# A node score repeated over the partitions: by TensorE transposes or by two transfers through DRAM

## The chip, the cores and the metric

The kernel runs on one core of a Trainium2 chip. The core has five engines that follow their own instruction streams in order: TensorE (PE; its weight loads are shown apart as PEld), VectorE (DVE), ScalarE (ACT), GpSimd (POOL) and SyncE (SP). SP computes nothing: it issues the transfers (DMAs) between DRAM and the on-chip memory SBUF. TensorE writes its products into PSUM[...]. The metric is the time of one execution in microseconds (us); less is better. The kernel before takes 1116.52 us, the median of three runs (1116.37 to 1117.14).

## The reference

The reference is a stack of four graph layers over 32 graphs of 512 nodes with 128 features, all with one 512 x 512 adjacency matrix `adj`. Each layer normalises its input, applies a relu, runs a graph layer and adds the result to `x`:

```python
h = jnp.maximum(_layernorm(x, axis=-1), 0.0)
x = x + _L0_gnn_ref(h, adj, ...)     # then L1, L2, L3 in the same way
```

Layers 1 and 2 are attention layers. Each node gets two scores, and the score of an edge is the sum of one score of each end. Layer 2, with layer 1 alike up to a weighting by `adj` and an MLP after it:

```python
Wh = jnp.einsum('bnf,fo->bno', h, W)
f1 = Wh @ a1
f2 = Wh @ a2
e = jax.nn.leaky_relu(f1[:, :, None] + f2[:, None, :], negative_slope=ALPHA)
e = jnp.where(adj[None, :, :] > 0, e, NEG_INF)
attention = jax.nn.softmax(e, axis=2)
```

Here `f2[:, None, :]` is the point of this study: one number per node, needed as a row beside every other node. Layer 0 has scores `u1`, `u2` and an index rule that pairs neighbouring nodes:

```python
e = u1[:, idx1] + u2[:, idx2]
e = jnp.where(e >= 0, e, ALPHA * e)
att = jax.nn.softmax(jnp.where(adj > 0, e, NEG_BIG), axis=1)
out = jnp.einsum('bik,bkl->bil', att, h) + x @ self_weight
```

Layer 3 has no scores that depend on the nodes: its attention is computed once from `adj`, and only two products per graph are left.

## The kernel before, in words

All of `x` stays in SBUF for the whole run, as `xs` with 128 partitions, 32 graphs, 4 chunks of 128 nodes and 128 features. Node n of a graph lies on partition n mod 128 of chunk n // 128. The masks made from `adj` (`bias`, `adjT`, `biasT`, `mask2T`, `adjTe`) and the weights stay in SBUF too. The work is one function per layer and graph: `layer0(b)` for all 32 graphs, then `layer1(b)` for all, then `layer2(b)` mixed with `layer3(b - 4)`.

Every layer begins with `preln(b)`: statistics on VectorE (L475, L477), the normalisation on GpSimd (L489, L510), four transposes on TensorE (L386) and a relu copy on ScalarE (L519), which gives `hT`. In layers 0 to 2, `project_scored` (L543) multiplies `hT` by a weight matrix with two more columns, so that `h` (copied by ScalarE at L377) holds 128 features and, in columns 128 and 129, the two scores of each node. A score is then a number on each of 128 partitions, for four chunks.

VectorE needs one of them as a row of 512 values, the same on every partition. `repeated` (L569) makes it with four TensorE transposes of a column that is read 128 times over; the result `prow` is a PSUM bank. In `attend` (layers 1 and 2) the four instructions at L587 add `prow` to the mask `bias`, write `y[0]` to `y[3]` and take the maximum of each row. ScalarE then adds the other score and applies the leaky relu (L612) and the exponential (L620). TensorE transposes the result, VectorE multiplies or copies it into `pT` (L629, L379), and TensorE forms the output `po` (L640). In `layer0` the row is made of `ls`, the leaky relu of the sum of both scores (`sc` and `ls`, L673 and L677, on VectorE). Two times two instructions at L692 add its even or odd nodes to `biasT`. Four transfers from SBUF to SBUF (L664) bring the other pairing of scores, `u`, into place; L702 is its first reader. ScalarE's exponentials are at L742, the scaled features `hs` and `hs2` at L770 and L771, the products at L776 and L784, and the sum into `xs` at L790.

The order of the instructions is found by `Plan` when the kernel is built. Each step is an `op` with an engine, an assumed length, what it reads and writes, and for a transfer its number of DMAs and an assumed load. `Plan.run` repeatedly takes the step that can begin first by these assumptions. Among steps of one engine that could begin within 0.05 us of each other it takes the one with the smaller `turn`, which is its graph's starting time plus four times the assumed length of the way to the step within the graph. After a step's end, 0.22 us (TensorE, ScalarE), 0.15 (VectorE), 0.13 (GpSimd) or 2.2 (SP) pass in the plan before its result can be read. At most seven graph layers are open at a time. Buffers are given out by the plan from pools: eight PSUM banks, five `scored` (for `h`), eight `scores` (for `y`), six `by_act` and others. Eight transfers can be on their way at once. The plan's order is fixed in the program: on each engine the instructions run in that order, so a waiting instruction holds up all that follow it on its engine. This includes SP, where a transfer that waits for its source holds up the transfers behind it.

`load_x(b + 6)` brings in the input of a later graph in layer 0 (L370), and `layer3` sends out the result (L909).

Of the kernel before, what the change touches and what calls it, by code (L numbers as in the profile page):

```python
# [33 lines left out]
P = 128  # L34
# [195 lines left out]
def kernel(  # L230
# [65 lines left out]
    scores = room("scores", 8, (P, C, P))  # L296
    turned = room("turned", 4, (P, C, P))
    spare = room("spare", 9, (P, C, P))

    plan = Plan(tc)  # L300
    op = plan.op
# [264 lines left out]
            )  # L566
        return h

    def repeated(col, reads):  # L569

        prow = value(banks, "prow")
        turn_op(lambda k: prow.t[:, k, :], lambda k: col(k).to_broadcast([P, P]), reads, [prow])
        return prow

    def attend(h, weights, v_weights):


        prow = repeated(lambda k: h[0].t[:, k, P + 1 : P2], h)
        y = [value(scores, "y") for _ in range(C)]
        rmax = Value()  # L580
        top = [Value() for _ in range(C)]
        for ib in range(C):

            def emit(ib=ib):
                if ib == 0:
                    rmax.own = small("rmax")
                nc.vector.tensor_tensor_reduce(  # L587
                    wide(y[ib].t), wide(prow.t), bias[:, ib, :], 1.0, LOWEST, ALU.add, ALU.max,
                    rmax.own[:, ib : ib + 1],
                )  # L590

            op(DVE, 0.61, emit, [prow, v_bias], [y[ib], top[ib]])
        ntop, nmax = Value(), Value()

        def emit_top():
# [56 lines left out]
    def layer0(b):  # L652
# [25 lines left out]

        dve(0.08, emit_sc, h, [sc])
        dve(0.08, emit_ls, [sc], [ls])  # L680
        prow = repeated(lambda k: ls.own[:, k : k + 1], [ls])
        y = [value(scores, "y") for _ in range(H)]
        rmax, top = Value(), [Value() for _ in range(H)]
        for hf in range(H):

            def emit_max(hf=hf):
                if hf == 0:
                    rmax.own = small("rmax")
                node = wide(prow.t).rearrange("p (i q) -> p q i", q=2)
                for k in range(2):  # L690
                    jb = 2 * hf + k
                    nc.vector.tensor_tensor_reduce(  # L692
                        wide(y[hf].t)[:, k * N2 : k * N2 + N2], node[:, hf, :], biasT[:, jb, :], 1.0, LOWEST,
                        ALU.add, ALU.max, rmax.own[:, jb : jb + 1],
                    )

            op(DVE, 0.7, emit_max, [prow, v_biasT], [y[hf], top[hf]])
        lt1, lt, nltm, nmax, ltn = (Value() for _ in range(5))

        def emit_lt1():  # L700
# [548 lines left out]
```

## Time and profile before

| | value |
|---|---|
| median of three runs | 1116.52 us |
| the profiled execution | 1114.53 us |
| its span, first to last instruction | 1112.8 us |
| TensorE, VectorE, ScalarE, GpSimd busy | 98%, 83%, 60%, 60% |
| `prow` on TensorE | 384 transposes, 273 ns each as recorded |
| first and last `prow` of layer 0 | 15.8 and 206.3 us |
| first and last `prow` of layers 1 and 2 | 212.0 and 1068.5 us |
| score instruction of layers 1 and 2 (L587) | 256 of 683 ns |
| score instruction of layer 0 (L692) | 128 of 415 ns |
| traffic of the transfers over the span | 20.50 MB in 56911 packets |

The profile is one execution recorded by the hardware. A group of instructions is written as line, engine, operation and output<-input; "x" is a count. Where instructions of TensorE overlap, the busy time of a group is less than the count times the mean. "SPq" is the issuing of a transfer by SP, and the time to landing of a transfer runs from its issue to the moment its data has arrived. A stage of the run is read from a view that gives every engine's busy time in a stretch of the span.

### The profile page before, as it was taken

How to read it: one execution, taken by the hardware profiler on the slowest of the kernel's cores; microseconds unless marked ns; L12 is line 12 of the kernel's file. 1: busy time of each engine (PE TensorE's matmuls, PEld its weight loads, DVE VectorE, ACT ScalarE, POOL GpSimd, SP SyncE). 2: the span in 40 equal slices, each digit the busy share in tenths (PEclk: the TensorE clock that was granted, in tenths of full speed). 3: DMA queues.
4: the chain of work that ended last, by engine and by line, in shares of the span. 5: the costliest groups of instructions: out<-in, count | busy, mean ns of one | idle time of the engine just before them, and what ended most of it. 6: DMA issues, size and time to landing. Idle time of an engine off the chain costs nothing.

```text
span 1112.8 us, 25144 instructions
## 1 busy us (share of the span) xinstructions
PE 1085.5 (98%) x8680; PEld 989.0 (89%) x8683; DVE 922.5 (83%) x3822; ACT 672.1 (60%) x1588; POOL 673.2 (60%) x1040
## 2 busy tenths in 40 slices
PE   5999999999999999999999999899999999999998
PEld 4899999998787877887788887899999999999997
DVE  8989899978889898998989897977777777777772
ACT  3456455567365565574656765866667766766661
POOL 8355454554546555646456555687776777777773
PEclk8899999999999999999999999999999999999999
DMA  7202210000000000000000000000100000000001
GB/s 189 58 11 50 43 36 2 2 2 2 1 1 1 1 1 1 1 1 1 1 1 2 1 1 1 1 20 20 30 21 20 21 20 20 20 21 29 21 21 39
DMA packets 56911, 20.50 MB, mean 18 GB/s; under 512 B 21584, under 2 KB 56272, under 8 KB 56784
## 3 DMA queue, kind: packets, MB, share of 16 engines
q1 hardware_dynamic: 56784, 18.90, 6.9%
q8 instruction: 69, 1.13, 0.4%
q14 instruction: 58, 0.48, 0.1%
HBM read 10.43 MB, written 8.39 MB: 17 GB/s over the span
## 4 chain that ended last, share of the span: by engine, by line
PE 75%; DVE 16%; ACT 3%; POOL 2%; issue 1%; SPq 1%; DMA 1%; POOLq 0%; ACTq 0%; DVEq 0%
PE po L640 16%; PE pt L386 13%; PE po L784 10%; PE po L901 10%; PE proj L557 6%; PE pg L834 5%; DVE y L587 4%; PE prow L386 3%; PE po L776 2%; ACT y L620 2%; DVE st L475 2%; PE po L897 2%; PE p L535 2%; DVE pT L629 2%; PE pz L535 1%
## 5 line engine op out<-in xcount | busy, mean ns | idle before, releaser
L640 PE MATMUL po<-h,pT 128*128 128x128 f32 x2048 | 244.2, 275 | 1.7 <-DVE pT L379 1.0
L510 POOL TENSOR_SCALAR xn<-xs,nmean,rstd 128x128 f32<-128x128 f32 x512 | 232.0, 469 | 19.7 <-DVE st L475 9.6
L640 PEld LDWEIGHTS po<-h,pT 128*128 128x128 f32 x2048 | 236.3, 192 | 5.8 <-issue 1.9
L620 ACT ACTIVATE y<-y,nmax 128x512 f32<-128x512 f32 x256 | 181.7, 712 | 41.1 <-DVE nmean L501 20.1
L612 ACT ACTIVATE y<-y,h 128x512 f32<-128x512 f32 x256 | 165.4, 712 | 37.4 <-DVE rmax L587 37.1
L489 POOL TENSOR_TENSOR rstd<-ve,mhalf 128x4 f32<-128x4 f32 x160 | 163.9, 1024 | 13.4
L587 DVE CUSTOM_DVE_ANT_0 y<-prow,bias 128x512 f32<-128x512 f32 x256 | 161.9, 683 | 9.5 <-PE prow L386 9.0
L519 ACT ACTIVATE hT<-pt 128x512 f32<-128x512 f32 x128 | 75.5, 591 | 125.0 <-PE pt L386 123.2
L386 PE MATMUL pt<-ident,y 128*128 128x128 f32 x1024 | 135.1, 274 | 2.5 <-ACT y L620 1.8
L901 PE MATMUL po<-h,offT 128*128 128x128 f32 x1024 | 135.4, 275 | 0.5 <-ACT h L377 0.5
L487 POOL TENSOR_SCALAR ve<-mv 128x4 f32<-128x4 f32 x160 | 36.7, 229 | 160.9 <-DVE rsum L756 57.7
L386 PEld LDWEIGHTS pt<-ident,y 128*128 128x128 f32 x1024 | 115.7, 141 | 20.0 <-ACT y L620 11.4
L834 PE MATMUL pg<-adjTe,hg 128*128 128x512 f32 x256 | 128.2, 593 | 0.0
L901 PEld LDWEIGHTS po<-h,offT 128*128 128x128 f32 x1024 | 124.6, 192 | 0.6 <-ACT h L377 0.6
L475 DVE BATCH_NORM_STATS2 st<-xs 128x6 f32<-128x128 f32 x512 | 109.9, 276 | 1.5 <-POOL xs L879 1.4
L557 PE MATMUL proj<-w_ext,hT 128*128 128x130 f32 x768 | 107.8, 279 | 2.3 <-ACT hT L519 2.3
L557 PEld LDWEIGHTS proj<-w_ext,hT 128*128 128x128 f32 x768 | 97.7, 194 | 6.7 <-ACT hT L519 2.9
L377 ACT COPY h<-proj 128x260 f32<-128x260 f32 x192 | 67.6, 371 | 46.3 <-PE proj L557 40.5
L879 POOL TENSOR_TENSOR xs<-xs,em 128x512 f32<-128x512 f32 x32 | 40.9, 1278 | 81.2 <-DVE em L878 81.2
L386 PE MATMUL pt<-ident,xn 128*128 128x128 f32 x512 | 85.2, 279 | 2.7 <-POOL xn L510 1.9
L629 DVE TENSOR_TENSOR pT<-pt,adjT 128x512 f32<-128x512 f32 x128 | 82.1, 680 | 3.4 <-PE pt L386 3.2
L742 ACT ACTIVATE y<-y,nmax 128x256 f32<-128x256 f32 x128 | 63.8, 501 | 31.1 <-DVE rs L760 14.0
(189 smaller groups left out, 2101.2 us busy)
## 6 DMA issues: line engine op xcount, KB each, us to landing
xs<-in_x_dram SPq DMA_DIRECT2D x32, 256.0 KB, 3.6
out_dram<-yo SPq DMA_DIRECT2D x32, 256.0 KB, 2.2
u<-h SPq DMA_DIRECT2D x128, 0.5 KB, 1.8
bias<-in_adj_dram SPq DMA_DIRECT2D x4, 256.0 KB, 3.3
wts<-in_L_gnn_W_dram SPq DMA_DIRECT2D x3, 64.0 KB, 3.8
rows<-in_L_gnn_bias_dram SPq DMA_DIRECT2D x2, 64.0 KB, 3.3
wt_o<-L_gnn_others_weight_dram SPq DMA_DIRECT2D x1, 64.0 KB, 2.3
wts<-n_L_gnn_self_weight_dram SPq DMA_DIRECT2D x1, 64.0 KB, 3.8
```

The lines of the kernel that those rows point to most:

```text
L386: nc.tensor.transpose(dst(k), src(k), ident)
L475: nc.vector.bn_stats(st[:, c, :], src(c))
L489: nc.gpsimd.tensor_tensor(rstd.own, ve, mhalf, ALU.pow)
L510: nc.gpsimd.tensor_scalar(xn.t[:, c, :], src[:, c, :], nmean.own[:, c : c + 1], rstd.own[:, c : c + 1], ALU.add, ALU.mult,)
L557: nc.tensor.matmul(p[:, c, :], lhsT=column(hT, 2 * k + c), rhs=w_ext, start=(b3 is None), stop=(b3 is None or c == 1),)
L587: nc.vector.tensor_tensor_reduce(wide(y[ib].t), wide(prow.t), bias[:, ib, :], 1.0, LOWEST, ALU.add, ALU.max, rmax.own[:, ib : ib + 1],)
L612: nc.scalar.activation(yw, yw, AF.Prelu, alpha=0.2, bias=h[0].t[:, ib, P : P + 1])
L620: nc.scalar.activation(yw, yw, AF.Exp, bias=nmax.own[:, ib : ib + 1], accum_out=ssum[0].own[:, ib : ib + 1])
L640: nc.tensor.matmul(po[ib].t[:, ib, :], lhsT=pT.t[:, jb, :], rhs=h[0].t[:, jb, 0:P], start=(jb == 0), stop=(jb == C - 1),)
L784: nc.tensor.matmul(po[ib].t[:, ib, :], lhsT=w, rhs=(hs if ib < H else hs2).t[:, jb, :], start=False, stop=(jb == C - 1),)
L834: nc.tensor.matmul(wide(pg.t), lhsT=hg.t[:, nb, :], rhs=adjTe[:, nb, :], start=(nb == 0), stop=(nb == C - 1))
L901: nc.tensor.matmul(po[ib].t[:, ib, :], lhsT=offT[:, jb, blk(ib)], rhs=h1.t[:, jb, :], start=False, stop=(jb == C - 1),)
```

## The change

`repeated` goes, and `repeat` comes in its place. It writes the score of the 512 nodes as one line of 2 KB into DRAM with SP, and reads that line back with a second transfer which repeats it over the 128 partitions. The destination is the last of the layer's `y` buffers, not a PSUM bank. The last score instruction then reads and writes the same buffer. For layer 0 the line is written with the even nodes first and the odd ones after (`step` is 2), by two transfers, so that the score instructions read contiguous halves. The DRAM lines come from a pool of eight.

```diff
+    dram = ctx.enter_context(tc.tile_pool(name="dram", bufs=8, space=bass.MemoryType.DRAM))
+    outside = Room(8, lambda n: dram.tile([1, N], F32, name=n, tag="row"))
...
-    def repeated(col, reads):
-
-        prow = value(banks, "prow")
-        turn_op(lambda k: prow.t[:, k, :], lambda k: col(k).to_broadcast([P, P]), reads, [prow])
-        return prow
+    def repeat(col, reads, v_row, step=1):
+
+        line = value(outside, "line")
+
+        def emit():
+            to = line.t.rearrange("o (q c p) -> q p (o c)", q=step, p=P // step)
+            for q in range(step):
+                nc.sync.dma_start(to[q], col()[q:P:step, :])
+
+        op(SP, 0.45 * step, emit, reads, [line], transfers=step)
+        op(SP, 0.45, lambda: nc.sync.dma_start(wide(v_row.t), line.t.to_broadcast([P, N])), [line], [v_row],
+           load=1.0, transfers=1)
...
-        prow = repeated(lambda k: h[0].t[:, k, P + 1 : P2], h)
         y = [value(scores, "y") for _ in range(C)]
+
+        repeat(lambda: h[0].t[:, :, P + 1], h, y[-1])
...
-                    wide(y[ib].t), wide(prow.t), bias[:, ib, :], 1.0, LOWEST, ALU.add, ALU.max,
+                    wide(y[ib].t), wide(y[-1].t), bias[:, ib, :], 1.0, LOWEST, ALU.add, ALU.max,
...
-            op(DVE, 0.61, emit, [prow, v_bias], [y[ib], top[ib]])
+            op(DVE, 0.61, emit, [y[-1], v_bias], [y[ib], top[ib]])
...
-        prow = repeated(lambda k: ls.own[:, k : k + 1], [ls])
         y = [value(scores, "y") for _ in range(H)]
+        repeat(lambda: ls.own, [ls], y[-1], 2)
...
-                node = wide(prow.t).rearrange("p (i q) -> p q i", q=2)
...
-                        wide(y[hf].t)[:, k * N2 : k * N2 + N2], node[:, hf, :], biasT[:, jb, :], 1.0, LOWEST,
+                        wide(y[hf].t)[:, k * N2 : k * N2 + N2], wide(y[-1].t)[:, hf * N2 : hf * N2 + N2], biasT[:, jb, :],
+                        1.0, LOWEST,
...
-            op(DVE, 0.7, emit_max, [prow, v_biasT], [y[hf], top[hf]])
+            op(DVE, 0.7, emit_max, [y[-1], v_biasT], [y[hf], top[hf]])
```

## The prediction

> **What bounds the kernel now.** I read the page's header first, then busy time by stage. I cut the stages where the node row `prow` changes form: `prow<-ident,ls` (layer 0) is last issued at 206.3 us, `prow<-ident,h` (layers 1 and 2) runs from 212.0 to 1068.5. Columns of the stage view: stretch, its length, busy us and instructions of PE, PEld, DVE, ACT, POOL, granted clock, DMA share, GB/s.
>
> ```profile
> PE 1085.5 (98%) x8680; PEld 989.0 (89%) x8683; DVE 922.5 (83%) x3822; ACT 672.1 (60%) x1588; POOL 673.2 (60%) x1040
> ...
> 60.00:211.00 151.00, 151.00 (x1358) 150.79 (x1357) 138.38 (x771) 84.50 (x307) 75.71 (x148) 1.00 0.15 26
> 211.00:672.00 461.00, 456.51 (x3246) 377.68 (x3247) 407.97 (x1599) 279.72 (x608) 249.90 (x345) 1.00 0.00 1
> 724.00:1112.80 388.80, 383.34 (x3394) 376.50 (x3392) 278.72 (x997) 247.97 (x524) 280.01 (x431) 1.00 0.08 23
> ```
>
> TensorE has no free time in any stage. VectorE is second: 92% in layer 0, 88% in layer 1, 72% in layers 2/3. The chain of waits, limited to layer 0, is TensorE alone, the row's transposes among it:
>
> ```profile
> by line: PE po L784 57.2%; PE proj L557 14.4%; PE po L776 14.3%; PE prow L386 7.0%; PE pt L386 6.9%; PE proj L552 0.2%
> ```
>
> In layers 2/3 TensorE's timeline repeats every 13.10 us (prow at 780.24 and 793.34), and the next work starts 0.43 us after a row does:
>
> ```profile
> 793.34 0.60 PE L386 MATMUL prow<-ident,h 128*128 128x128 f32 x4
> 793.77 1.06 PE L535 MATMUL p<-wts,hT 128*128 128x128 f32 x8
> ```
>
> So a row costs TensorE about 0.435 us of its order, not the 4 x 273 ns that the records show, which overlap. Layer 0 repeats every 6.24 us (`h` copied at 115.37, 121.60, 127.84). Last, SP's timeline, since the change puts its work there:
>
> ```profile
> 116.02 2.86 SPq L664 DMA_DIRECT2D u<-h  x4
> 118.93 0.59 SPq L370 DMA_DIRECT2D xs<-in_x_dram  x1
> 122.26 2.55 SPq L664 DMA_DIRECT2D u<-h  x4
> ...
> xs<-in_x_dram SPq DMA_DIRECT2D x32, 256.0 KB, 3.6
> out_dram<-yo SPq DMA_DIRECT2D x32, 256.0 KB, 2.2
> u<-h SPq DMA_DIRECT2D x128, 0.5 KB, 1.8
> ```
>
> The reader should see that one DMA issue holds SP for about 0.635 us (2.55/4), so layer 0 already uses 2.55+0.6 = 3.15 of each 6.24 us of SP.
>
> **What the Trainium skill says.** "DMA: Bandwidth & Descriptors", section on the anatomy of one DMA: a transfer has a fixed cost of about 2 us, most of it the receipt from the memory written, heaviest for HBM. The trace agrees: 1.8 us for 0.5 KB SBUF to SBUF, 2.2 for 256 KB into DRAM. Same page, rules for kernel authors: a DMA that reads what another wrote must wait for its semaphore, and a strided last dimension becomes one descriptor per element. The line is therefore 512 elements of 4 bytes and the second transfer cannot start before the first has landed. Same page, specifications: below 512 B the engine does a read-modify-write. No run of before writes small elements into DRAM. Same page, queues and rings: each engine consumes a ring in order, so a small write queued behind an x load waits for it; u's landing, 1.8 median but 3.7 at most, would fit.
>
> **The change part by part.**
>
> *Removed from TensorE.* 96 rows (32 in each of three layers) x 0.435 = 41.8 us, 13.9 a layer. Every stage is TensorE's, so this is the largest possible gain, if nothing else takes its place. A PSUM bank per row comes free too; I price that at 0, as TensorE does not wait for banks in the steady stages.
>
> *VectorE.* The same 256 + 128 score instructions read SBUF instead of PSUM. Rows with both operands in SBUF: 686 ns (em, L878) to 718 (xs<-res, L855), against 683 now; so 0 to +35 ns, at most 9 us on L587 and some 4 on L692. I take 0; the 8% to 28% of VectorE that is idle hides it, and uncovered it would cost those 13 us. Using the last `y` in place orders the last score instruction behind the others; they run in that order already.
>
> *Added to SP and DRAM.* Layers 1 and 2: one write (0.635 of SP), a wait for landing, one broadcast (0.635). Layer 0: two writes of 256 elements, one broadcast, 3 x 0.635 = 1.9. Landing L of the line: 1.8 (u) to 3.7 (u's worst); I take 2.1, near out's 2.2. Landing of the broadcast, 256 KB into SBUF: 2.2 (out) to 3.6 (x load); I take 2.8. From `h` to the row in place: 2.1 + 2.8 = 4.9 us with no queueing, and 7.3 at the upper ends.
>
> *Who waits.* On VectorE the score instruction waits for the broadcast, and behind it stand the pT products and copies of other layers that TensorE needs. Layers 2/3: `h` is complete at 787.05 (786.23 + 0.82) and its scores start at 795.10: 8.05 us are there already. Layer 1: `h` complete at 524.10 or before, scores at 525.74, but the first half of `h` is copied at 520.04; the order must move by some 3 us, for which five `scored` and eight `scores` buffers leave room at 13.6 us a layer. The plan charges 0.45+2.2+0.45+2.2+1.0 = 6.3 us for the path, so it orders VectorE's work for a later row than my 4.9. In layers 2/3 SP's only other transfer is `out`, whose source is ready at 791.83; the write (787.1) and broadcast (near 789.8) go ahead of it.
>
> *Layer 0 on SP.* The broadcast waits on SP, and behind it are the next layer's four u transfers (for L702) and x load. SP's cycle: four u 2.54, first write 0.635, L from the second write's issue to its landing, broadcast 0.635: 3.81 + L = 5.9 with L = 2.1, if the x load is issued in that wait; 6.55 if it lies elsewhere in the order (only until x's last load at 156 us). TensorE would want 6.24 - 0.435 = 5.8, VectorE 6.24 x 0.92 = 5.7. So SP takes the bound over; at 5.9 for some layers and 6.55 for others, layer 0 gains -0.34 x 16 = -5 and loses 0.3 x 16 = +5. The crowded SP start (35 to 50 us, u transfers back to back) is inside that. I take 0 for layer 0.
>
> *Sum.* Layers 2/3: -13.9, less the ends where TensorE is not full (383.34 of 388.80, and the handover from layer 1): -12.5. Layer 1: VectorE would go from 88.5% to 91%, and its chain passes often between engines; I take two thirds, -9. Layer 0: 0. Total -21.5. The profiled execution ran 1114.53 with a span of 1112.8; this gives a span of 1091.3 and a run near 1093. Its 1.7 us outside the span stay. The median, 1116.52, lies 2.0 above the profiled run, so 1095.
>
> **Rivals.**
> *A. SP becomes the bound of layer 0 and takes more than the rest gives (slower).* If the 4-byte writes into DRAM land in L = 3.6 (as slow as an x load), the cycle is 7.4 with the x load inside, 8.05 outside: +1.2 to +1.8 over 6.24, x 32 = +38 to +58, less 21.5: 1133 to 1153. It decides from 3.81 + L = 6.24 + 21.5/32 = 6.9, that is L = 3.1 (2.5 with the x load outside). For it: SP already spends half of layer 0, and small DRAM writes are unpriced. Against it: the two small landings seen are 1.8 and 2.2.
> *B. VectorE bounds layers 0 and 1 (little gained).* Layer 0 has 0.5 us of VectorE slack in 6.24, layer 1 1.6 in 14.4; a row late by a microsecond eats it. Then only layers 2/3 give: 1116.5 - 12.5 = 1104, and with the 13 us of slower score reads, 1117. For it: VectorE's 92%. Against it: in layers 2/3 it cannot happen at 72%.
> *C. The order changes for the worse.* Longer planned paths defer everything behind the row, by 4 x 4.64 us of planned turn in layers 1 and 2 (0.45+2.2+0.45+2.2 for 0.44+0.22, times the planner's 4), so more layers are open at once and buffers run out; a stall of 0.5 us in each of 96 layers would cost 48 us against the 41.8 saved, about 1122. Nothing in the trace shows buffers short, so little weight.
>
> **How the numbers follow.** Forecast 0.50 (1080 to 1104); A 0.29, slower; B 0.14, 0.10 of it faster and 0.04 within no change; C 0.07, 0.03 unchanged and 0.04 slower. That is faster 0.60, same 0.07, slower 0.33, where 0.2% (2.2 us) is about what a measurement of this kernel can tell. Forecast's own range 1080 to 1104. Up to 1135 takes in B, C and A's lower end; below 1080 (nearly the whole 41.8) I leave 0.06, above 1135 0.13.
>
> **What would show it.** The 13.10 us period of layers 2/3 becomes about 12.67; if it does not, C or a late row holds. The line's landing is near 2.1 us and the broadcast's near 2.8; the 6.24 us of layer 0 becomes 5.9 to 6.5. Line landings above 3 us, SP without pause in layer 0 and TensorE idle before `po` there show A. VectorE above 97% in layer 0 shows B. If scores wait for the broadcast in layers 1 and 2 by more than a microsecond each, my landing prices were wrong and so is the forecast.

## The result and the profile after

The changed kernel takes 1698.76 us, the median of four runs (1695.66 to 1701.41), against 1116.44 us for the kernel before on the same chip. The ratio is 1.521 (95% interval 1.519 to 1.524), so the change costs 582 us where a gain of 21.5 was forecast. The profiled execution took 1699.38 us with a span of 1697.7.

The header of the page of the changed kernel, busy time by engine:

```profile
PE 1235.4 (73%) x8299; PEld 1103.1 (65%) x8299; DVE 935.6 (55%) x3822; ACT 680.1 (40%) x1588; POOL 696.3 (41%) x1040
```

No engine is full any more. TensorE was 98% busy before. It executes 8299 matmuls instead of 8680, and its busy time is nevertheless longer, 1235.4 us for 1085.5. The next view shows the reason. These are stages of the changed kernel, with the columns of the stage view in the prediction: layer 0, then layer 1 with the first graphs of layer 2, then the rest of layers 2/3 from 1300 us on.

```profile
60.00:365.00 305.00, 216.19 (x1431) 199.79 (x1430) 162.62 (x873) 93.79 (x333) 95.78 (x158) 0.81 0.33 42
365.00:1060.00 695.00, 524.73 (x3253) 427.63 (x3254) 435.09 (x1693) 306.57 (x658) 280.57 (x379) 0.86 0.11 15
1300.00:1697.00 397.00, 286.09 (x2137) 278.16 (x2134) 181.63 (x635) 156.69 (x330) 177.29 (x271) 0.85 0.13 27
```

The granted clock (the third number from the end) is 0.81 to 0.86, where it was 1.00 in the stages shown before, and a matmul that is left takes longer: those of `po` from `pT` (L650) take 295 ns, for 275 before. In the profiled runs of this case the mean clock goes with TensorE's busy share: 0.994 at 98% before, 0.931 at 87% and 0.875 at 78% in two kernels of the experiments (`unread`, `l0_turn`), 0.841 at 73% here. That the idle time comes first is seen in experiment 6: with the same instructions in the same order, another shape of the line's write takes the share from 75% to 94% and the clock from 0.861 to 0.985. The second to last number is the share of time that the DMA engines are busy: 11% in layer 1. Little is being moved there while TensorE, VectorE and ScalarE wait.

The last row of layer 0 was begun at 206.3 us before (its transposes) and at 363.8 now (its write), which is 157.5 us later. From there to the end of the span it takes 1333.9 us instead of 906.5, which is 427 more. So about a quarter of the loss is in layer 0 and three quarters come after it. The chain of work that ended last, by line:

```profile
DMA line<-h 20%; DMA y<-line 18%; DMA line<-ls 9%; PE po L650 6%; PE pt L388 5%; PE po L911 4%; DVE y L597 4%; PE proj L559 3%; PE p L537 2%; PE pg L844 2%; DMA u<-h 2%; DVE st L477 1%; POOL xn L512 1%; ACT y L622 1%; ACT h L379 1%
```

Before, layer 0's chain was TensorE alone. Now the three kinds of transfer that the change adds carry 47% of the chain of the whole run, and the write (`line`) weighs more than the broadcast. Who waits for them is in the view of waits. First VectorE's waits (in total us, times, longest):

```profile
DVE y L597 <- DMA y<-line: 388.3, 58, 15.3
DVE y L701 <- DMA y<-line: 95.6, 26, 10.3
DVE lt L712 <- DMA u<-h: 68.5, 16, 8.0
```

Then SP's own waits:

```profile
SPq L581 <- DMA line<-h: 576.4, 64, 12.6
SPq L581 <- DMA line<-ls: 144.1, 27, 8.8
```

In layers 1 and 2, 58 of 64 graphs find VectorE waiting for the row, 6.7 us each. On SP the broadcast (L581) waits for the line, 9.0 us each time in layers 1 and 2. In layer 0 what is queued behind it on SP, the next layer's `u` transfers, comes late as well: that is the 68.5 us of L712.

One graph of layers 2/3 shows the length of the path. SP's timeline (start, duration):

```profile
1228.78 0.36 SPq L578 DMA_DIRECT2D line<-h  x1
1237.38 0.33 SPq L581 DMA_DIRECT2D y<-line  x1
```

and VectorE's timeline at the end of the same path, with the idle time before it in brackets:

```profile
1242.26 0.69 DVE L597 CUSTOM_DVE_ANT_0 y<-y,bias 128x512 f32<-128x512 f32 x1 [6.26 <-DMA y<-line]
```

The line took 8.6 us from its issue until SP could issue the broadcast, and the broadcast another 4.9 us until the row could be used. That is 13.5 us from `h` to the row, against 4.9 forecast, 6.3 assumed by the plan and 7.3 for the two upper ends of my bounds. Behind L597 on VectorE stand the copies and products that TensorE needs; TensorE's next work after this wait was a matmul at 1244.86, after 6.51 us without any: it waited for `hT` from ScalarE, which waited for a VectorE product (`own`) that stands behind L597.

Layer 0 shows the same write on SP's timeline:

```profile
212.42 0.33 SPq L581 DMA_DIRECT2D y<-line  x1
212.84 2.56 SPq L674 DMA_DIRECT2D u<-h  x4
215.50 1.26 SPq L578 DMA_DIRECT2D line<-ls  x2
216.80 0.60 SPq L372 DMA_DIRECT2D xs<-in_x_dram  x1
225.00 0.33 SPq L581 DMA_DIRECT2D y<-line  x1
```

From broadcast to broadcast it takes 12.58 us. SP issues for 4.8 of these and then stands until the line has landed, with nothing of the later layers going past.

### The profile page after: what moved, and what is told of

It reads as the page before. It is cut to its first block, busy times and chain, and to the rows that moved or that the text cites. A ratio compares the mean times of both kernels' runs of the same rounds, so it can differ in the third digit from the quotient of the medians.

```text
span 1697.7 us, 24773 instructions
## 1 busy us (share of the span) xinstructions
PE 1235.4 (73%) x8299; PEld 1103.1 (65%) x8299; DVE 935.6 (55%) x3822; ACT 680.1 (40%) x1588; POOL 696.3 (41%) x1040
## 4 chain that ended last, share of the span: by engine, by line
DMA 50%; PE 27%; DVE 11%; ACT 4%; issue 3%; POOL 3%; SPq 2%; ACTq 0%; DVEq 0%; POOLq 0%
DMA line<-h 20%; DMA y<-line 18%; DMA line<-ls 9%; PE po L650 6%; PE pt L388 5%; PE po L911 4%; DVE y L597 4%; PE proj L559 3%; PE p L537 2%; PE pg L844 2%; DMA u<-h 2%; DVE st L477 1%; POOL xn L512 1%; ACT y L622 1%; ACT h L379 1%
## 5 line engine op out<-in xcount | busy, mean ns | idle before, releaser
L597 DVE CUSTOM_DVE_ANT_0 y<-y,bias 128x512 f32<-128x512 f32 x256 | 174.1, 708 | 389.8 <-DMA y<-line 388.3
L650 PE MATMUL po<-h,pT 128*128 128x128 f32 x2048 | 281.6, 295 | 59.4 <-DVE pT L639 44.0
L650 PEld LDWEIGHTS po<-h,pT 128*128 128x128 f32 x2048 | 270.3, 212 | 67.7 <-DVE pT L639 38.2
L512 POOL TENSOR_SCALAR xn<-xs,nmean,rstd 128x128 f32<-128x128 f32 x512 | 250.6, 503 | 97.2 <-DVE nmean L503 28.9
L559 PE MATMUL proj<-w_ext,hT 128*128 128x130 f32 x768 | 136.3, 328 | 46.7 <-ACT hT L521 46.0
L491 POOL TENSOR_TENSOR rstd<-ve,mhalf 128x4 f32<-128x4 f32 x160 | 164.1, 1026 | 13.3
L388 PE MATMUL pt<-ident,xn 128*128 128x128 f32 x512 | 109.3, 319 | 76.5 <-POOL xn L512 67.5
L559 PEld LDWEIGHTS proj<-w_ext,hT 128*128 128x128 f32 x768 | 124.7, 240 | 56.0 <-ACT hT L521 51.8
L388 PEld LDWEIGHTS pt<-ident,xn 128*128 128x128 f32 x512 | 72.2, 158 | 103.8 <-POOL xn L512 95.1
L537 PE MATMUL p<-wts,hT 128*128 128x128 f32 x256 | 53.4, 374 | 109.4 <-ACT hT L521 109.4
L537 PEld LDWEIGHTS p<-wts,hT 128*128 128x128 f32 x256 | 46.3, 272 | 114.0 <-ACT hT L521 113.9
```

Of the source, the lines that this page charges most:

```text
L388: nc.tensor.transpose(dst(k), src(k), ident)
L491: nc.gpsimd.tensor_tensor(rstd.own, ve, mhalf, ALU.pow)
L512: nc.gpsimd.tensor_scalar(xn.t[:, c, :], src[:, c, :], nmean.own[:, c : c + 1], rstd.own[:, c : c + 1], ALU.add, ALU.mult,)
L537: nc.tensor.matmul(pt.t[:, c, :], lhsT=column(hT, c), rhs=w, start=(b3 is None), stop=(b3 is None or c == C - 1),)
L559: nc.tensor.matmul(p[:, c, :], lhsT=column(hT, 2 * k + c), rhs=w_ext, start=(b3 is None), stop=(b3 is None or c == 1),)
L597: nc.vector.tensor_tensor_reduce(wide(y[ib].t), wide(y[-1].t), bias[:, ib, :], 1.0, LOWEST, ALU.add, ALU.max, rmax.own[:, ib : ib + 1],)
```

## The experiments

### 1. Are the transfers themselves that slow?

The first kernel leaves the graph layers out. It holds only transfers of these shapes, in seven chains that write a line and read it back six times each.

```diff
+    for _ in range(REP):
+        nc.sync.dma_start(to_row(la), col)
+        repeat(ra, la)
...
+    for _ in range(REP):
+        nc.sync.dma_start(ld.rearrange("o (p c) -> p (o c)", p=P), sc)
+        repeat(rd, ld)
```

> The graph layers are left out: the kernel loads x, sends it out again as the output, and in between runs seven chains of transfers, each chain six times write and read back, nothing beside them. Shape of the write: (a) 512 elements of 4 bytes into one DRAM line of 2 KB, as the change does in layers 1 and 2; (b) 256 of them, as in layer 0; (c) 128; (d) 128 pieces of 16 bytes; (e) 512 elements of 4 bytes, each 512 bytes from the next in DRAM; (f) 512 elements of 4 bytes from SBUF to SBUF; (g) four transfers of 128 elements. Theory 'the transfer is slow in itself': (a) takes about 8.4 us from issue to the next issue that waits for it, as in the changed kernel, and the broadcast 3.3 to 4.9. Rival 'slow only beside the other traffic and SP's queue': (a) takes about 2.1, as I had priced it. Which part of (a) is slow: by element count, (b) is about 5, (c) about 3.5 and (d) like (c); by neighbours sharing a piece of DRAM, (e) is about 3 while (a) is 8.4; by DRAM as such, (f) is about 2.5 and (e) like (a).

It took 266.43 us, and its landings are long everywhere: 9.5 us for the 512 pieces of 4 bytes, but also 13.3 for 128 pieces of 16 bytes and 13.7 for spaced ones. The chains used buffers of their own and ran among each other, so a landing contains the queue of the others. It is inconclusive on what a write costs by itself.

The second one leaves the graph layers out as well and makes every transfer wait for the one before it, so nothing else is under way.

```diff
-        nc.sync.dma_start(to_row(la), col)
-        repeat(ra, la)
+        dma(to_row(la), col)
+        dma(row, all_of(la))
```

> As in the first probe the graph layers are left out and x goes through unchanged, but now every transfer waits for the one before it, so that nothing runs beside it. Five times each, write and read back: (a) 512 elements of 4 bytes into one DRAM line of 2 KB; (b) 256 of them; (c) 128; (d) 128 pieces of 16 bytes; (e) 512 elements of 4 bytes, each 512 bytes from the next in DRAM; (f) 512 elements of 4 bytes from SBUF to SBUF; (g) the line in one piece from one partition; (i) 512 elements of 4 bytes, the four of a partition side by side. If the slowness is in the small writes to DRAM themselves, (a) takes about 8 us to the next issue and (g) about 2.2. By count of elements: (b) 5, (c) 3.5, (e), (f) and (i) like (a), (d) like (c). By writers of different engines sharing a piece of DRAM: (e) and (i) about 3, (f) about 2.5, (d) between. By DRAM as such: (f) about 2.5 with (e) and (i) at 8. If (a) takes about 2.1, the slowness comes from what runs beside it.

It took 381.48 us. Since SP issues a transfer when the former has landed, the time between two starts on SP's timeline is issue to landing. The table has the median of the last four of five (the first of a shape took longer). A pair of the shape of the change (`la`), one of 16-byte pieces (`ld`), and one of 4-byte pieces 512 bytes apart in DRAM (`le`):

```profile
60.16 0.36 SPq L42 DMA_DIRECT2D la<-h  x1
68.66 0.33 SPq L42 DMA_DIRECT2D row<-la  x1
...
221.83 0.32 SPq L42 DMA_DIRECT2D ld<-sc  x1
223.24 0.32 SPq L42 DMA_DIRECT2D row<-ld  x1
...
257.34 0.36 SPq L42 DMA_DIRECT2D le<-h  x1
259.13 0.36 SPq L42 DMA_DIRECT2D row<-le  x1
```

| write | issue to landing |
|---|---|
| 512 pieces of 4 bytes, adjacent in DRAM (as in layers 1 and 2) | 8.5 us |
| 256 such pieces (one of layer 0's two) | 7.3 |
| 128 such pieces | 7.2 |
| 512 such pieces, the four of a partition side by side | 7 to 9 |
| 512 pieces of 4 bytes, 512 bytes apart in DRAM | 1.8 |
| 512 pieces of 4 bytes, SBUF to SBUF | 2.0 |
| 128 pieces of 16 bytes, adjacent in DRAM | 1.4 |
| 2 KB in one piece | 1.15 |

So the 8.5 us are there without any other work. It is not the count of pieces (512 spaced ones take 1.8, 128 adjacent ones 7.2), nor the size of 4 bytes alone, nor DRAM as such. It is pieces of 4 bytes that lie next to each other in DRAM; only one wider spacing, 512 bytes, was tried. The closest pair in the table is the four pieces of a partition side by side (7 to 9 us) and the pieces of 16 bytes (1.4 us): both fill the same 2 KB of DRAM in the same order, and only the size of the pieces, and with it their number, differs. The Trainium skill, "DMA: Bandwidth & Descriptors", section on why small descriptors are slow, says that only transfers with HBM pay for small pieces and that SBUF to SBUF doesn't. The 2.0 against 8.5 us agree; the 1.8 us of the spaced pieces, which go to DRAM too, do not follow from the per-packet costs named there. The read-modify-write that I quoted in the prediction would fit a cost between neighbours, but the pieces of 16 bytes lie next to each other too, are also below 512 bytes, and took 1.4 us. No run here looks inside the DMA engines, so the mechanism stays open.

The broadcast of the same 256 KB took 5.0 us after `la`, 4.1 after `ld` and 3.1 after the line written in one piece. Why it depends on how the line was written is open too.

### 2. Layer 0 alone put back

Layer 0 gets its transposes again; layers 1 and 2 keep the transfers.

```diff
-        repeat(lambda: ls.own, [ls], y[-1], 2)
+        prow = repeated(lambda k: ls.own[:, k : k + 1], [ls])
...
-            op(DVE, 0.7, emit_max, [y[-1], v_biasT], [y[hf], top[hf]])
+            op(DVE, 0.7, emit_max, [prow, v_biasT], [y[hf], top[hf]])
```

> Layer 0 keeps its transposes; layers 1 and 2 use the transfers. Theory 'landing comes later than the fixed order assumes, and VectorE waits for the row in every layer': the loss stays in layers 1 and 2, which lost some 245 us (211 to 672 became 365 to 1060) and 160 us (672 to 1112 became 1060 to 1698 with the clock lower), so about 1500 to 1550 us. Rival 'SP's cycle of layer 0 is the cause' (case A of the prediction): about 1095, since layers 1 and 2 have SP nearly to themselves.

It took 1540.5 us, within the first theory's range, so layer 0's part of the loss is 158 us, as the two traces had it, and 424 remain. The wait of VectorE in layers 1 and 2 is what it was:

```profile
DVE y L603 <- DMA y<-line: 379.4, 62, 16.9
```

The landings, in this kernel's list of DMA issues (KB each, median us to landing):

```profile
y<-line SPq DMA_DIRECT2D x64, 256.0 KB, 4.8
...
line<-h SPq DMA_DIRECT2D x64, 2.0 KB, 8.8
```

### 3. The transfers made, the row not used

This is the kernel before, with its transposes and with the added transfers; the row goes to a buffer that nothing reads. What this adds is the work on SP and on the DMA queues alone.

```diff
+    unread = room("unread", 1, (P, C, P))
...
+        repeat(lambda: h[0].t[:, :, P + 1], h, value(unread, "row"))
...
+        repeat(lambda: ls.own, [ls], value(unread, "row"), 2)
```

> The kernel before, transposes and all, with the lines written and broadcast beside them into a buffer that nothing reads. Theory 'VectorE's wait for the row is what costs': layers 1 to 3 as before, and layer 0 only as slow as u, queued on SP behind a broadcast that waits for its line, makes it: 12 us a layer at worst, so 1120 to 1300. Rival 'the traffic or SP itself slows everything': above 1400.

It took 1305.48 us, just above the range expected for the first theory (one timed execution, as of the two probes and of `l0_turn` and `retimed`), against 1118.67 for the kernel before beside it. Layers 1 to 3 cost 12 us more than before (first to last `prow` of layers 1 and 2: 390.8 to 1259.5, that is 868.7 us against 856.5). Layer 0 costs 179 us more: the first `prow` of layer 1 moves from 212.0 to 390.8. There, SP has one cycle per graph:

```profile
208.12 0.33 SPq L589 DMA_DIRECT2D row<-line  x1
...
220.34 0.33 SPq L589 DMA_DIRECT2D row<-line  x1
```

12.2 us, and 32 of them are 391 us, which is the end of layer 0. So in layer 0 SP's order does the harm, without anyone reading the row; what is late is `u`, for which VectorE waited 190.4 us. In layers 1 and 2 the transfers alone do almost none, and there it must be the reader that pays.

### 4. The plan told how late the row comes

This is the changed kernel, with 6.0 us added to the write's landing and 1.0 to the broadcast's in the plan.

```diff
-        op(SP, 0.45 * step, emit, reads, [line], transfers=step)
+        op(SP, 0.45 * step, emit, reads, [line], transfers=step, lag=6.0)
...
-           load=1.0, transfers=1)
+           load=1.0, transfers=1, lag=1.0)
...
-            done = end + DELAY[op.engine]
+            done = end + DELAY[op.engine] + op.lag
```

> The changed kernel, with only the plan's assumption corrected: 6.0 us added to the landing of a line and 1.0 us to that of a broadcast, so that the order is made for 8.65 and 4.65 us. Theory 'the fixed order assumes a row too early': most of the loss comes back, 1100 to 1250 us. Rival 'the latency itself cannot be hidden, buffers and open layers run out': above 1450 us. Rival 'SP in order': layer 0 stays above 9 us a layer, its 300 us keep some 100 over before, and layers 1 to 3 recover.

It took 1349.12 us: more comes back than the second theory allows, less than the first expected, and layer 0 stays at some 10 us a graph, as the third has it. VectorE's wait for the row in layers 1 and 2 falls from 388.3 us to 61.6, and the time after the last row of layer 0 (336.2 to 1347.4 us) is 1011 us instead of 1334, where it was 906.5 before. So three quarters of the later loss (323 of 427 us) go away when the order is no longer made for a row that comes after 6.3 us. Layer 0 gains only 28 us: there the order on SP, not the reader's place, is the limit.

### 5. The same order with larger pieces

In `packed`, a score line is written as 128 pieces of 16 bytes, the four scores of a partition together (ScalarE brings the four of `h` side by side first, 0.18 us). The line is then in another order, which VectorE undoes with its access pattern. `single` has the same buffers and the same order of instructions on every engine, with 512 pieces of 4 bytes. `packed12` has the larger pieces in layers 1 and 2 only, and transposes in layer 0.

```diff
 # packed
+        op(SP, 0.45, lambda: nc.sync.dma_start(line.t.rearrange("o (p c) -> p (o c)", p=P), four()), reads, [line],
+           transfers=1)
...
-                    wide(y[ib].t), wide(y[-1].t), bias[:, ib, :], 1.0, LOWEST, ALU.add, ALU.max,
+                    y[ib].t, wide(row.t).rearrange("p (i c) -> p c i", c=C),
 # single against packed
-        op(SP, 0.45, lambda: nc.sync.dma_start(line.t.rearrange("o (p c) -> p (o c)", p=P), four()), reads, [line],
+        op(SP, 0.45, lambda: nc.sync.dma_start(line.t.rearrange("o (c p) -> p (o c)", p=P), four()), reads, [line],
-                    y[ib].t, wide(row.t).rearrange("p (i c) -> p c i", c=C),
+                    y[ib].t, wide(row.t).rearrange("p (c i) -> p c i", c=C),
```

> As the change, in all three layers, but the line is written as 128 pieces of 16 bytes (a node's partition first, its chunk second) instead of 512 or 2 x 256 pieces of 4. In layers 1 and 2 ScalarE first puts a partition's four scores side by side (some 0.19 us); the row goes into a buffer of its own, of which there are two, and VectorE reads it with a step of 16 bytes. In the serial probe this write took 1.4 us and its broadcast 4.1, together 5.5, under the 6.3 that the plan assumes. Theory 'what costs is the landing of the 4-byte writes against an order made for 6.3 us': all of the loss goes and TensorE is full again, 1075 to 1105 us. Rival 'a trip through DRAM by SP is too slow for this order in any form': above 1150 us.

> The same as the kernel with 16-byte pieces, in the same order on every engine and with the same buffers, but the line is written as 512 pieces of 4 bytes, chunk first, as in the change (one transfer, in layer 0 too). Theory as above: 8.5 + 5.0 us a row bring the loss back, 1500 to 1750 us. Rival 'the separate row buffer, the gathered scores and the different order are what helps': within 50 us of the kernel with 16-byte pieces.

> As the kernel with 16-byte pieces, but layer 0 keeps its transposes and its u transfers stay alone on SP. It saves TensorE 2 x 13.9 us at most. If SP costs nothing in layer 0 when the writes are quick, it is some 5 to 14 us slower than the kernel with all three layers changed (1085 to 1105 us); if SP still binds layer 0, it is the faster of the two.

`single` took 1632.01 us (one timed execution), `packed` 1265.81 (ratio to before 1.134, 1.130 to 1.137), `packed12` 1251.05 (1.122, 1.119 to 1.124). The groups of score instructions (busy us, mean ns, idle before them and its releaser), of `single`:

```profile
L601 DVE CUSTOM_DVE_ANT_0 y<-row,bias 128x512 f32<-128x512 f32 x256 | 166.5, 701 | 328.3 <-DMA row<-line 324.2 <-PE po L800 4.2
```

and of `packed`:

```profile
L601 DVE CUSTOM_DVE_ANT_0 y<-row,bias 128x512 f32<-128x512 f32 x256 | 290.5, 1188 | 5.1 <-PE po L800 2.8 <-DMA row<-line 2.3
```

With the larger pieces the wait for the row is gone: 324.2 us become 2.3. In `packed` the lines land in 1.4 us and the row in 3.9 (medians of its DMA issues), 5.3 us together, and the plan's 6.3 us for the path is then long enough. Layer 0 hardly suffers any more, as `packed12`, which undoes the change there, is only 1.2% faster. Most of that 1.2% is not SP's either: the last line of layer 0 is written at 228.3 us in `packed` and at 216.0 in the kernel of the next experiment, which has the same transfers.

But `packed` and `packed12` were expected at 1105 us or less and miss that by some 150. VectorE now needs 1188 ns per score instruction, 1105 in the median, for 683 before. It reads the row with a step of 16 bytes, and 256 times the 505 ns by which the mean has risen are 129 us, on an engine that had 190 us to spare over the whole run. So `packed` has a second cost. The next experiment takes the step away.

### 6. The same, read without the step

This is `packed` with VectorE's access to the row changed (L601, and L706 alike): it reads the row in the order in which it lies. The instructions and their order are the same; the scores reach the wrong nodes.

```diff
-                    y[ib].t, wide(row.t).rearrange("p (i c) -> p c i", c=C),
+                    y[ib].t, wide(row.t).rearrange("p (c i) -> p c i", c=C),
```

> The kernel with 16-byte pieces, in the same order on every engine and with the same transfers, but VectorE reads the row with a step of 4 bytes instead of 16 (layer 0: instead of 32). The scores then reach the wrong nodes; as much work is done as before. In the kernel with 16-byte pieces the score instruction took 1105 ns against 683 (layer 0: 612 against 415), which is 256 x 0.42 + 128 x 0.20 = 133 us of VectorE, and nothing waited for rows. Theory 'that step is all that keeps it above the kernel before': instructions back at 690 and 415 ns and 1075 to 1110 us, with layer 0 near 6 us. Rival 'SP or the landing still binds': 1130 us or more, with SP waits ahead of VectorE's.

It took 1150.99 us (ratio 1.031, 1.029 to 1.033). Against `single`, which reads in the same way and differs only in how the line is written, this is 481 us less. `single` is 515 us slower than before, so the size of the pieces in one small write, with the broadcast that gets slower after it, explains 93% of it. This share and the three quarters of experiment 4 are not parts of one sum: the wait comes from a late row in an order made for an early one, and either remedy removes most of it.

It is still 3.1% slower than before and above the 1110 us that the first theory allowed, but no SP wait holds it: the row is there in time (VectorE waited 2.3 us for it in layers 1 and 2), and TensorE is busy for 1076.1 us instead of 1085.5. VectorE's timeline shows a first score instruction of 1.24 us, and then three of 0.68:

```profile
908.63 1.24 DVE L601 CUSTOM_DVE_ANT_0 y<-row,bias 128x512 f32<-128x512 f32 x1
...
909.81 0.68 DVE L601 CUSTOM_DVE_ANT_0 y<-row,bias 128x512 f32<-128x512 f32 x1
```

GpSimd's timeline in the same time:

```profile
908.06 1.27 POOL L889 TENSOR_TENSOR v<-v,rows 128x512 f32<-128x512 f32 x1
```

The slow score instruction ends at 909.87, 0.54 us after GpSimd's at 909.33, so most of its own work lies after that. The Trainium skill, "SBUF — State Buffer", section on who interferes with whom, says that a VectorE instruction with two SBUF inputs contends with a GpSimd instruction that reads SBUF, and that one of the two then waits. Before, one input was the PSUM bank `prow`. This page bears on the change, and I had not used it. The traces agree: here 38 of the 256 score instructions took over 0.8 us, and all 38 began while a GpSimd instruction was running. In the kernel before, with the row in PSUM, 108 of 256 began beside one too, and none took over 0.7 us.

### 7. The row read from SBUF, with no transfer at all

This is the kernel before, its transposes kept; ScalarE copies `prow` to an SBUF buffer (96 copies of 580 ns), and VectorE reads that.

```diff
-        return prow
+        row = value(rows_in, "row")
+        copy_op(ACT, 0.49, lambda: row.t, lambda: prow.t, [prow], [row])
+        return row
```

> The kernel before without any new transfer: the row is transposed as before, and ScalarE copies it from PSUM into one of two SBUF buffers (0.58 us, 96 times), from where VectorE reads it. Theory 'two operands from SBUF against GpSimd': the score instruction takes 740 to 790 ns on average instead of 683 and the kernel 1125 to 1165 us. Rival 'the loss has to do with the transfers or their order': 1117 to 1125 us and 690 ns.

It took 1170.75 us (ratio 1.048, 1.045 to 1.051): 4.8% with no transfer added, a little above the range expected. The groups of GpSimd's normalisation and of the score instructions:

```profile
L511 POOL TENSOR_SCALAR xn<-xs,nmean,rstd 128x128 f32<-128x128 f32 x512 | 303.4, 606 | 16.6 <-DVE ve L809 6.5 <-DVE nmax L605 4.8 <-DVE ltn L722 0.3
...
L590 DVE CUSTOM_DVE_ANT_0 y<-row,bias 128x512 f32<-128x512 f32 x256 | 181.5, 752 | 5.3 <-ACT row L378 5.0 <-PE po L787 0.3
```

The mean of L590 is 752 ns with a median of 684 and a longest of 1764: most are as fast as before, and some wait for GpSimd: 19 took over 0.8 us, and all 19 began while a GpSimd instruction was running (so did 140 of the other 237, so not every meeting costs). GpSimd's `xn` rises from 469 to 606 ns, 512 times, so it is the other one that waits more often: 70 us of its time against VectorE's 18. Both theories of the SBUF read, a slower read and a lock between two engines, are told apart by the median, which does not move, and by where the long ones lie. ScalarE's copy is in this price too, and one `spare` buffer less, which made room for the row; how much of the 4.8% these are wasn't separated.

### 8. The row kept out of VectorE's SBUF reads

`packed_psum` is `packed`, with ScalarE copying the row into a PSUM bank in the right order. `psum_told` tells the plan that this copy takes 1.1 us and not 0.55. `four_rows12` makes four rows of 128 scores with one TensorE transpose and writes 4 pieces of 512 bytes, in layers 1 and 2; the row is read from SBUF. `four_psum12` is that with ScalarE's copy into PSUM.

```diff
 # packed_psum
+        prow = value(banks, "prow")
+        copy_op(ACT, 0.55, lambda: prow.t, lambda: wide(row.t).rearrange("p (i c) -> p c i", c=C), [row], [prow])
 # psum_told
+        copy_op(ACT, 1.1, lambda: prow.t, lambda: wide(row.t).rearrange("p (i c) -> p c i", c=C), [row], [prow])
 # four_rows12
+        op(PE, 0.11, lambda: nc.tensor.transpose(pt.t[0:C, 0, :], col(), ident), reads, [pt])
+        copy_op(ACT, 0.25, lambda: four.t, lambda: pt.t[0:C, 0, :], [pt], [four])
+        op(SP, 0.45, lambda: nc.sync.dma_start(line.t.rearrange("o (c p) -> (o c) p", c=C), four.t), [four], [line],
+           transfers=1)
 # four_psum12, besides
+        copy_op(ACT, 0.49, lambda: prow.t, lambda: v_row.t, [v_row], [prow])
```

> Layer 0 as before. In layers 1 and 2 one transpose turns the 128 x 4 scores into 4 rows of 128, ScalarE copies them to SBUF, four pieces of 512 bytes go to the DRAM line in the order of the nodes, and the broadcast brings the line back into the last y buffer. TensorE keeps 1 of 4 transposes, so at most 64 x 0.33 = 21 us can be saved. With the write at 1.2 us and the broadcast at 3.1 to 4 the row is there before the order wants it: 1092 to 1110 us. Rival 'the longer planned path leaves VectorE or TensorE short of ready work': 1117 us or more.

> All three layers through DRAM with 16-byte pieces; ScalarE then copies the row, in the order of the nodes, into a PSUM bank (I assume 0.55 us, 96 times), and the score instructions read that bank as before. Theory 'with quick writes the rest is lost because VectorE reads two operands from SBUF, which it cannot do while GpSimd reads SBUF': score instructions back at 683 and 415 ns on average, no xn of GpSimd above some 1.3 us, and 1075 to 1110 us. Rival 'the rest is lost in the order that the plan makes of a longer path': 1125 us or more.

> The kernel with 16-byte pieces and ScalarE's copy into PSUM, with the plan told that the copy takes the 1.1 us that it took instead of 0.55. If VectorE's 36 us of waiting for that copy is what holds it above the kernel before: 1085 to 1115 us. If the order for a later row is: still 1125 to 1150 us.

> Layers 1 and 2 with one transpose to four rows of 128, four pieces of 512 bytes into DRAM, broadcast, and ScalarE's copy (0.58 us) into PSUM in the order of the nodes; layer 0 as before. Its sister without the copy took 1.0445 of the time before, with score instructions of 758 ns. Theory 'two operands from SBUF' alone: 1095 to 1117 us. If the order for a later row costs as well: 1120 to 1150 us.

| kernel | median us | ratio to before (95%) | score instruction, mean ns | `xn` on GpSimd, mean ns |
|---|---|---|---|---|
| before | 1116.4 to 1117.2 | 1 | 683 | 469 |
| `four_rows12` (SBUF) | 1166.63 | 1.045 (1.043 to 1.046) | 758 | 501 |
| `four_psum12` (PSUM) | 1132.95 | 1.015 (1.014 to 1.016) | 681 | 472 |
| `packed_psum` | 1143.68 | 1.024 (1.022 to 1.026) | 684 | 481 |
| `psum_told` | 1124.76 | 1.008 (1.006 to 1.009) | 682 | 486 |

With the row in PSUM, score instructions and `xn` are as fast as before or nearly so, and `four_psum12` is 34 us faster than `four_rows12` although ScalarE has one copy per graph more. The small pieces, an order made for too early a row and the read from SBUF are three costs of the change; with all three answered, what is left of the loss is 0.8% in `psum_told`. All four kernels are slower than their first theories had them (1117 us at most). Three lie where the rivals put them, by which the order for a longer path costs as well, and `psum_told` just below that; experiment 9 tries the order alone. TensorE has less to do in it (1064.3 us busy, 95% of the span, for 1085.5) and it still gains nothing. In it VectorE waits for ScalarE's copy, which has become the last step of the path:

```profile
DVE y L603 <- ACT prow L380: 27.5, 23, 5.2
```

### 9. The order alone

This is the kernel before with the same instructions, the plan being told that the transposes' result comes 5.64 us later.

```diff
-                op.way = max(op.way, n.way + n.length + DELAY[n.engine])
+                op.way = max(op.way, n.way + n.length + DELAY[n.engine] + n.lag)
...
-            done = end + DELAY[op.engine]
+            done = end + DELAY[op.engine] + op.lag
...
-        turn_op(lambda k: prow.t[:, k, :], lambda k: col(k).to_broadcast([P, P]), reads, [prow])
+        op(PE, 0.44, emit, reads, [prow], lag=5.64)
```

> The kernel before, instruction for instruction, but ordered as if a transposed row came 5.64 us later than it does, so 6.3 us after its step begins, which is what the plan assumes of the trip through DRAM. No transfer is added. If the order for a later row is what costs once the writes are quick, this kernel loses too: 1130 to 1170 us (a PSUM bank per row is held those microseconds longer in the plan, which belongs to it). If the order is innocent: 1114 to 1122 us.

It took 1134.44 us (ratio 1.016, 1.015 to 1.017). VectorE does not wait for the row here; all its idle time before the score instructions of layers 1 and 2 is 0.3 us. An order that is made for a later row costs 18 us by itself. The PSUM bank is held longer in this plan too, so a part of it may belong to the bank.

None of these kernels is faster than the one before.

## Why the prediction was wrong, by its own steps

**What bounds the kernel before.** This reading stands. TensorE was full, and 41.8 us was the largest gain. Where the row comes in time, TensorE's busy time does fall: by 21 us in `psum_told`, at a mean granted clock of 0.978 for 0.994 before. Busy time multiplied by clock falls from 1079 to 1041 us, by 38, which as a rough reckoning is nearly the 41.8.

**Landing of the line.** This is the step that failed: "Landing L of the line: 1.8 (u) to 3.7 (u's worst); I take 2.1". It was 8.5 us, far above both bounds. Both bounds came from `u`, which stays in SBUF, and the value from `out`, which goes into DRAM in pieces of 512 bytes. I had written that the line is 512 elements of 4 bytes, that below 512 bytes a read-modify-write is done and that no run of before writes small elements into DRAM, and then bounded it by rows that do not. The fixed cost of about 2 us that I quoted from "DMA: Bandwidth & Descriptors" is given there, in the section on the anatomy of one DMA, for transfers that GpSimd issues; SP's other small writes in `probe_serial` are near it or below (1.15 to 2.0 us), the adjacent 4-byte ones are not. `single` against `packed_flat` puts 481 us on this term, the slower broadcast after such a write included.

**Landing of the broadcast.** 2.8 taken, 2.2 to 3.6 as bounds. It was 4.8 (median of `l0_turn`), and 3.9 after larger pieces. This size was too small by 1 to 2 us, which was second to the write.

**Who waits.** The mechanism was right as put: L597 waits, and behind it stands TensorE's supply. The size failed with the landings. The order of the kernel before gave the row 8.05 us after `h` in layers 2/3 and the path is 13.5, so 5.5 us are missing; the trace shows a wait of 6.26 us in the graph above and 6.7 on average. The comparison of 4.9 us with the plan's 6.3 would have been the right one with the right landing, and `retimed` shows that most of the later loss turns on it.

**Layer 0 on SP.** The cycle of 3.81 + L was right in form. In the graph shown above, 8.9 us pass from the second write's issue (216.1 us) to the broadcast's (225.0), and 3.81 + 8.9 is 12.7, for 12.58 measured; `unread` shows 12.2. I had taken 0 for layer 0, and it cost about 158 us. The price of 0.635 us of SP for every issue held for these writes (0.63) but not for a broadcast (0.33) or the write of 512 pieces (0.37); this error is small and went the other way.

**VectorE's score instructions.** "I take 0", with at most 13 us. Here a second step failed, independent of the first. The rows that I compared, `em` and `xs<-res`, have two SBUF inputs and take 686 to 718 ns, so I read them as the price of an SBUF input. What the experiments show is not a price per read, but waiting between VectorE and GpSimd: 4.8% in `copied_row`, with its ScalarE copies. `em` was a poor neighbour, since GpSimd mostly stood idle beside it: 27 of its 32 instructions met none of GpSimd's, and GpSimd's next one, L879, waits for it (81.2 us of idle before L879). The other neighbour had the sign in it. The shortest, median and longest of `xs<-res` in the kernel before, in ns:

```profile
L855 DVE SCALAR_TENSOR_TENSOR xs<-res,xs x32: 653/684/1262, 296.1 to 718.3; 128x512 f32<-128x512 f32 x32
```

I had read its mean, 718 ns, as a price. The median is 684, and four of the 32 took over 0.8 us, all beside GpSimd. In the changed kernel this cost hides behind the waits: L597 has a mean of 708 ns, and 7 of 256 took over 0.8 us.

**PSUM bank at 0.** No experiment gave the bank alone.

**Rival A** had the right place, the right sign and the right point of decision, L = 3.1. It allowed only L = 3.6 and so gave 1133 to 1153. It also left layers 1 and 2 their full gain of 21.5, although the same landing makes VectorE wait there, and that is the larger part of the loss. **Rival B** did not come about: VectorE is 55% busy. `packed` comes nearest to it, with VectorE at 84% and its score instructions at 1188 ns. **Rival C**, to which I gave 0.07, is real: `lagged` has its price without the transfers, 18 us, where I had allowed 48 for it.

**What would show it.** The last sign named there came: scores that wait for the broadcast in layers 1 and 2 by more than a microsecond, here 6.7 us each in 58 of 64 graphs. The period of layers 2/3, forecast at 12.67 us, became 20.6 (mean distance of their broadcasts). The chances were wrong for a plain reason: slower had 0.33 while the deciding transfer had no row in the trace, and the range ended at 1135 because an unknown was given a known's bounds.

**Still open.** Why adjacent pieces of 4 bytes take 7 to 9 us. Why the broadcast is quicker after a line written in one piece. And how the rest of the loss in `retimed` (105 us after layer 0 over before) and in `psum_told` (0.8%) divides between the order, ScalarE's work and the waits.

## What to carry to other kernels

A transfer is priced by the shape of its pieces at both ends, not by its bytes: if the trace has no row with pieces of that size going to that memory, its landing is unknown and the range must show that. Where a value comes by a longer path, compare the path with what the order assumes and count what stands behind the waiting reader on every in-order queue, SP's too. And before an operand moves from PSUM to SBUF, look at what GpSimd reads at that time, and read the longest of a group beside its mean.

## What was not expected of the hardware

- A write of 128 pieces of 4 bytes that are adjacent in DRAM took 7.2 us; four times as many bytes in 128 pieces of 16 took 1.4, and 512 pieces of 4 bytes spaced by 512 bytes took 1.8.
- The broadcast of the same 2 KB line over 128 partitions took 5.0, 4.1 or 3.1 us, by how the line had been written.
- A VectorE instruction that reads a row in SBUF with a step of 16 bytes took 1105 ns in the median (`packed`) instead of 681 without the step (`packed_flat`); ScalarE's copy of the row into PSUM with that step took 1098 ns (`packed_psum`) instead of 593 without (`four_psum12`).
- A few VectorE instructions with two SBUF inputs took up to 1.76 us beside GpSimd, with the median unchanged at 684 ns (`copied_row`); all that took over 0.8 us began while a GpSimd instruction ran, 19 here and 38 in `packed_flat`.
